# A decoder layer's feed forward in three exact bfloat16 products, behind a survey of the weights, with two key block sets

## The chip, the cores and the metric

The kernel runs on one core of a Trainium2 chip. A core has TensorE (PE, with its weight loads shown apart as PEld), VectorE (DVE), ScalarE (ACT), GpSimd (POOL) and SyncE (SP), which here issues nearly all DMAs. Each engine works through its own queue of instructions in order. The metric is the device time in microseconds (us) of one execution. Lower is better.

## The reference, cut to what matters

One decoder layer on `x` of shape (2, 1024, 256) in float32: causal self attention with rotary embedding, cross attention to 77 context rows, and a gated feed forward. Each is added to its input and followed by a layer norm. All weights of the feed forward are drawn from {-1, 0, 1}; `setup_inputs` multiplies them by 8, and each output row has a float32 scale.

```
x = layernorm(x + self_attention(x))            # 16 heads of 16, causal, rotary
x = layernorm(x + cross_attention(x, ctx))      # ctx: (2, 77, 256)
tlin(x, w, s) = einsum('bsi,oi->bso', x, w) * s
h = silu(tlin(x, w1_w, w1_s)) * tlin(x, w2_w, w2_s)   # 256 -> 1024
h = gelu(tlin(h, h1_w, h1_s))                          # 1024 -> 1024
h = gelu(tlin(h, h2_w, h2_s))                          # 1024 -> 1024
x = layernorm(x + tlin(h, w3_w, w3_s))                 # 1024 -> 256

_ternary(key, shape) = jax.random.randint(key, shape, -1, 2).astype(float32)
factors = {..., 'L0_ffn_w1_w': 8.0, ..., 'L0_ffn_w3_w': 8.0, ...}
```

## The kernel before, in words

Tokens are cut into tiles of 128 (8 per batch) and tiles into five chunks, `CHUNKS` = (batch, first tile, tiles): (0,0,2), (0,2,2), (1,0,4), (0,4,4), (1,4,4). A chunk passes through these steps, each a Python generator whose `yield` gives a pace in microseconds:

- `start` / `project` (L257): per tile, transposes, the query, key and value products, the rotary step on VectorE into a padded tile `qk_pad` (two of them in turn), transposes back. Keys and values go to tiles `kT` and `v` per block of 512 keys, from a pool of 3.
- `top` / `maxima` (L320): scores of each query tile against its earlier keys into the one scores bank `su` (four PSUM banks of 512), and a VectorE reduction (L353) of that bank. The next scores wait for it. The maxima are added to the queries, so the exponentials later need no subtraction.
- `weighted` / `values` (L364): per head group and key tile, transposed scores into `su`, ScalarE's exponential (L400), GpSimd's causal select on the diagonal (L403), and the product with the values into `po`. The value products of one key tile are issued behind the scores of the next.
- `rest`: `self_finish` (L420: division, output projection, residual, norm) and `cross` (L433: the same again on 77 context rows, with its own maxima L461 and exponentials L482).
- `fed` / `feed_forward` (L506): the gate and up layers (tiles `pg`, `pu`), two hidden layers and the last one (`pf`), all with float32 operands. A chunk's weights come as 22 slices of 512 KB from HBM, 5 buffers deep.

The set of scores matmuls for four heads uses four groups of 32 rows of the array at once (`tiled`, L72). All matmuls of the attention are recorded by the helper at L69, those of the feed forward by the helper at L83.

The order is written by hand. `start(0)`, `top(0)`, `weighted(0)` and `cross_keys` (L152) run first, then `rest(0)` beside `start(1)` (`together`, L580: steps are taken by pace). From there on `beside` (L592) takes the attention step by step: maxima of chunk 1, values of chunk 1, then the rest of chunk n together with start and maxima of chunk n+1, values of n+1, and so on. After each step it places feed-forward instructions ("filler") worth the step's pace. The feed forward of a chunk can only begin when its `rest` is done (`attended`), and chunks are fed in order. Filler matmuls may stand at most `AHEAD` = 2 steps ahead of the attention. When the attention is at its end the remaining feed forward runs alone.

Pace of a scores bank in `maxima` is 2.6; of a full key tile in `values` 1.4; of a product of 512 columns in the feed forward 0.86.

## Time and profile before

| | before |
|---|---|
| median of 3 runs | 1361.11 us (1361.1 to 1364.54) |
| the profiled execution, its own time | 1359.41 us |
| its span, first to last instruction | 1357.7 us |
| mean granted TensorE clock | 0.932 |
| busy PE / DVE / ACT / POOL | 1245.1 / 455.4 / 304.9 / 84.0 us |
| DMA moved | 66.19 MB, 14.3% of the span on SP's and ACT's main queue |

How to read the profile: the page has the busy time of each engine, the chain of work that ended last with its shares by engine, groups of instructions by line, operation and shape with their mean, and DMA issues. A float32 matmul appears as two records, each with its own weight load. A busy time can overlap that of the next instruction by the pipeline's depth, so busy times of short groups add up to a little more than the time that they fill. "Stretches" below are a table of the engines' busy time in windows of the span, with the clock that the throttle granted to TensorE (1.00 is full speed).

The first feed-forward matmul starts at 142.4 us, and the last attention matmul ends at 1161.8 us.

### The profile page before, as it was taken

Reading aid. Unit: us, or ns where it says so; the run is one execution under the profiler, and the core shown is the slowest. Engines: PE = TensorE matmul, PEld = TensorE weight load, DVE = VectorE, ACT = ScalarE, POOL = GpSimd, SP = SyncE. Lnnn points to the kernel's source line nnn. Section 1 sums busy time; section 2 is a strip of 40 time slices with the busy share of each in tenths; the row PEclk is TensorE's granted clock in tenths of the full one; section 3 lists DMA queues with packets and bytes.
Section 4 is the critical chain, followed back from the end, with each engine's and each line's share of the span. In section 5 each row is a group of like instructions: output and inputs, shape, how many; then the busy total and the mean of one; then the engine's idle time right before and its main releaser. Section 6 shows DMA issues by size and latency. Waiting matters only on the chain.

```text
span 1357.7 us, 15205 instructions
## 1 busy us (share of the span) xinstructions
PE 1245.1 (92%) x6672; PEld 638.9 (47%) x6672; DVE 455.4 (34%) x705; ACT 304.9 (22%) x328; POOL 84.0 (6%) x131
## 2 busy tenths in 40 slices
PE   6978998898999999998989999899899798999997
PEld 3554646675466755432225544543222343554445
DVE  3133603346133347750003334686000232140002
ACT  1211151211431121004452212010444303011110
POOL 2110011000211000000011000000000000000000
PEclk7585899898899899999999989899899998999999
DMA  5010211122111112110000000111000000122220
GB/s 161 32 47 0 78 48 47 48 78 85 47 61 49 63 47 70 47 63 16 32 31 17 31 31 32 47 47 47 32 31 17 32 26 22 62 92 72 73 74 15
DMA packets 24594, 66.19 MB, mean 49 GB/s; under 512 B 4328, under 2 KB 9553, under 8 KB 24529
## 3 DMA queue, kind: packets, MB, share of 16 engines
q1 hardware_dynamic: 24257, 64.44, 14.3%
q8 instruction: 52, 0.85, 0.3%
q10 hardware_dynamic: 272, 0.79, 0.2%
q14 instruction: 13, 0.11, 0.0%
HBM read 63.12 MB, written 2.10 MB: 48 GB/s over the span
## 4 chain that ended last, share of the span: by engine, by line
PE 82%; ACT 7%; DVE 7%; POOL 2%; issue 2%; DMA 1%; SPq 0%; POOLq 0%; ACTq 0%; DVEq 0%
PE pf L83 36%; PE su L69 18%; PE pm L69 7%; PE po L69 6%; PE pg L83 4%; PE pu L83 4%; ACT pr L400 3%; DVE part L353 2%; PE pq L69 2%; PE pt L226 1%; ACT pr L482 1%; PE pt L235 1%; PE pt L300 1%; DVE top L461 1%; PE pt L246 1%
## 5 line engine op out<-in xcount | busy, mean ns | idle before, releaser
L83 PE MATMUL pf<-nxt,wf 128*128 128x512 f32 (+1 forms) x640 | 251.1, 535 | 0.0
L83 PE MATMUL pf<-hid,wf 128*128 128x512 f32 (+1 forms) x640 | 249.8, 524 | 0.0
L353 DVE TENSOR_REDUCE part<-su 128x4 f32<-128x2048 f32 (+3 forms) x76 | 165.5, 2178 | 76.2 <-PE su L69 75.8
L400 ACT ACTIVATE pr<-su 128x2048 f32<-128x2048 f32 (+1 forms) x104 | 140.6, 1352 | 208.9 <-PE su L69 208.7
L83 PEld LDWEIGHTS pf<-hid,wf 128*128 128x128 f32 x640 | 113.4, 190 | 119.8 <-issue 114.3
L83 PEld LDWEIGHTS pf<-nxt,wf 128*128 128x128 f32 x640 | 122.0, 201 | 98.5 <-issue 91.1
L69 PE MATMUL su<-q,kT 17*128 17x512 f32 (+3 forms) x832 | 97.7, 538 | 26.7 <-ACT pr L400 24.8
L69 PE MATMUL su<-kT,q 16*128 16x128 f32 (+3 forms) x1152 | 92.3, 434 | 12.4 <-DVE part L353 12.1
L546 DVE TENSOR_SCALAR nxt<-pf,sc 128x256 f32<-128x256 f32 (+1 forms) x64 | 39.4, 615 | 181.6 <-PE pf L83 181.0
L69 PE MATMUL po<-pr,v 128*32 128x512 f32 (+3 forms) x832 | 90.5, 510 | 2.0 <-POOL pr L403 1.5
L69 PEld LDWEIGHTS su<-q,kT 17*128 17x128 f32 x832 | 35.6, 197 | 90.1 <-ACT pr L400 59.1
L417 DVE COPY osb<-po 128x512 f32<-128x512 f32 (+1 forms) x20 | 11.7, 585 | 186.7 <-PE po L69 186.7
L403 POOL TENSOR_SCALAR_AFFINE_SELECT pr<-pr 128x512 f32<-128x512 f32 x64 | 40.6, 635 | 513.6 <-ACT pr L400 513.6
L69 PEld LDWEIGHTS su<-kT,q 16*128 16x128 f32 x1152 | 45.7, 205 | 51.9 <-DVE part L353 25.9
L83 PE MATMUL pg<-xTc,wf 128*128 128x512 f32 (+1 forms) x160 | 69.2, 552 | 0.3 <-DVE xTc L218 0.3
L83 PE MATMUL pu<-xTc,wf 128*128 128x512 f32 (+1 forms) x160 | 65.8, 530 | 0.1
L530 ACT ACTIVATE gate<-pg,sc 128x512 f32<-128x512 f32 (+1 forms) x40 | 24.1, 601 | 185.2 <-PE pg L83 185.1
L83 PE MATMUL pf<-wf,nxt 128*128 128x256 f32 x256 | 58.4, 385 | 0.0
L548 ACT ACTIVATE nxt<-nxt 128x1024 f32<-128x1024 f32 (+1 forms) x16 | 23.7, 1483 | 134.1 <-DVE nxt L546 133.9
L83 PEld LDWEIGHTS pf<-wf,nxt 128*128 128x128 f32 x256 | 48.7, 193 | 9.0 <-issue 1.6
L565 DVE TENSOR_TENSOR o<-pf,s 128x256 f32<-128x256 f32 x16 | 6.8, 423 | 134.8 <-PE pf L83 134.8
L482 ACT ACTIVATE pr<-su 77x2048 f32<-77x2048 f32 (+1 forms) x20 | 30.6, 1531 | 64.2 <-PE su L69 64.2
(103 smaller groups left out, 1018.9 us busy)
## 6 DMA issues: line engine op xcount, KB each, us to landing
wf<-in_wf_dram SPq DMA_DIRECT2D x110, 512.0 KB, 3.2
x<-in_x_dram SPq DMA_DIRECT2D x16, 128.0 KB, 3.4
out_dram<-x SPq DMA_DIRECT2D x16, 128.0 KB, 1.8
wqkv<-in_w_qkv_dram ACTq DMA_DIRECT2D x1, 768.0 KB, 4.9
wk<-in_wkT_dram SPq DMA_DIRECT2D x1, 512.0 KB, 5.2
wq<-in_wqT_dram SPq DMA_DIRECT2D x1, 512.0 KB, 3.5
rope<-in_rope_dram SPq DMA_DIRECT2D x1, 256.0 KB, 5.1
wproj<-in_w_proj_dram SPq DMA_DIRECT2D x1, 256.0 KB, 5.0
```

The costliest lines, as they stand in the source:

```text
L69: latest[0] = nc.tensor.matmul(*args, **kw).ins
L83: ins = nc.tensor.matmul(*args, **kw).ins
L226: nc.tensor.transpose(pt[:, g * P : (g + 1) * P], m_pad[:, 4 * g : 4 * g + 4, :].rearrange("p h d -> p (h d)"), ident)
L235: nc.tensor.transpose(pt[:, g * P : (g + 1) * P], osb[:, g, i * P : (i + 1) * P], ident)
L246: nc.tensor.transpose(pt[:, k * P : (k + 1) * P], y[:, k * P : (k + 1) * P], ident)
L353: nc.vector.tensor_reduce(part[:, m, g0 : g0 + gm, :].rearrange("p g j -> p j g"), su[:, :, : gm * r].rearrange("p j (g r) -> p j g r", g=gm),
L400: nc.scalar.activation(pr[:, :, q0:], su[:, :, q0 : n * P], AF.Exp)
L403: nc.gpsimd.affine_select(out=pr[:, :, q0 : q0 + P], in_=pr[:, :, q0 : q0 + P], compare_op=ALU.is_ge, fill=0.0, base=0, pattern=[[0, 4], [ ...
L482: nc.scalar.activation(pr[:L], su[:L, :, : n * P], AF.Exp)
L530: nc.scalar.activation(gate, pg, AF.Tanh, scale=sc[:, 0, f : f + 1])
L546: nc.vector.tensor_scalar(nxt[:, f, :], pf, sc[:, s, f : f + 1], None, ALU.mult)
L548: nc.scalar.activation(nxt[:, f - 3 : f + 1, :], nxt[:, f - 3 : f + 1, :], AF.Gelu)
```

## The change

- **Survey.** While the first chunk's attention runs, all 22 weight slices are loaded once. VectorE takes the maximum of the low 16 bits of every float32 word (L704 of the changed kernel), ScalarE copies the high 16 bits as a bfloat16 tile (L706), and SP stores that to a scratch tensor `wh` in HBM (L707). One matmul against ones and a comparison turn the maxima into a flag: 0 if every weight is exact in bfloat16.
- **Branch.** Every engine loads the flag (L800) and branches (L815). On 0 it runs `feed_forward_exact`, else the float32 `feed_forward`. All that stands behind, the attention of the chunks from 1 on included, is in both sides; pools for it are opened anew inside each side (`part`).
- **Three products.** Activations x stay float32 in `hid`; `split` takes the upper half-word as the first bfloat16 plane, subtracts it on VectorE (L606), copies the upper half of what is left into a bfloat16 tile on ScalarE (L608), and writes the last remainder into the lower half-words of x (L609). The three planes sum to x. Each float32 matmul becomes three bfloat16 ones with the same weight block, of which the first and last plane are read in steps of four bytes. Where a layer begins (`first`) two outputs are summed together, the early blocks first, then plane by plane.
- **Pace.** A pair of bfloat16 products has the pace 0.43 for 512 columns, so the filler is again placed by its time.
- **Order and buffers.** The chunks are now (0,0,2), (0,2,2), (0,4,4), (1,0,4), (1,4,4). Keys and values have two fixed sets (`kT`, `v`), used by one batch and then by the other. Queries have two fixed tiles, and cross attention's queries `qx` take the tile of the chunk's own queries. There is one `qk_pad` instead of two.

```diff
-CHUNKS = ((0, 0, 2), (0, 2, 2), (1, 0, 4), (0, 4, 4), (1, 4, 4))
+CHUNKS = ((0, 0, 2), (0, 2, 2), (0, 4, 4), (1, 0, 4), (1, 4, 4))
...
-    for i in range(2):
+    for i in range(1):
         pad = wself.tile([P, 2, H, 32], F32, name=f"qk_pad{i}")
...
-    kT, v = {}, {}
+    kT = [keys.tile([P, NG, KB], F32, name=f"kT{i}") for i in range(NT // KT)]
+    v = [keys.tile([P, KT, H * DV + 16], F32, name=f"v{i}") for i in range(NT // KT)]
+    for i in range(NT // KT):
+        nc.gpsimd.memset(v[i], 1.0)
+    qs = [queries.tile([P, NG, KB], F32, name=f"q{i}") for i in range(2)]
...
-    def cross(b, t0, n):
+    def cross(b, t0, n, qx):
         x1T = yield from transposed_tokens(b, t0, n)
-        qx = queries.tile([P, NG, n * P], F32, tag="q", name="qx")
...
+    def word_halves(x):
+        both = x.bitcast(BF16).rearrange("p k (n two) -> p k n two", two=2)
+        return both[..., 1], both[..., 0]
+
+    def planes_of(x, mid):
+        upper, lower = word_halves(x)
+        return upper, mid, lower
+
+    def split(x, mid, k0, k1):
+
+        upper, lower = word_halves(x)
+        left = pl.acts.tile([P, k1 - k0, x.shape[-1]], F32, tag="left", name="left", bufs=2)
+        nc.vector.tensor_tensor(left, x[:, k0:k1, :], upper[:, k0:k1, :], ALU.subtract)
+        left_upper = word_halves(left)[0]
+        nc.scalar.copy(mid[:, k0:k1, :], left_upper)
+        nc.vector.tensor_tensor(lower[:, k0:k1, :], left, left_upper, ALU.subtract)
+
+    def planes_summed(sums, K, step, first):
+
+        if first:
+            early = K // 2 if K > KC else 0
+            runs = [[(p, k) for k in range(early) for p in range(3)]] if early else []
+            runs += [[(p, k) for k in range(early, K)] for p in range(3)]
+        else:
+            runs = [[(p, k) for k in range(K) for p in range(3)]]
+        for r, products in enumerate(runs):
+            for ps, operands in sums:
+                for m, (p, k) in enumerate(products):
+                    filling(
+                        ps,
+                        *operands(p, k),
...
+                    )
+                    if m % 2:
+                        yield 2 * step
+
+    def feed_forward_exact(b, t0, n, alone):
+        slices = slices_of(wh, BF16)
+        N = n * P
+        step = 0.215 * n / KT
+        x2T = yield from transposed_tokens(b, t0, n)
+        xmid = pl.acts.tile([P, KC, N], BF16, tag="xmid", name="xmid")
+        split(x2T, xmid, 0, KC)
+        planes = planes_of(x2T, xmid)
...
+        for f in range(FC):
...
+            for group in [sums] if f == 0 else [[x] for x in sums]:
+                yield from planes_summed(group, KC, step, f == 0)
+            gated(pg, pu, hid, f)
+            if f % 2:
+                split(hid, mid, f - 1, f + 1)
+        for s in (2, 3):
...
+                yield from planes_summed(sums, FC, step, f0 == 0)
+                for f, (pf, _) in zip(fs, sums):
+                    hidden(pf, nxt, s, f, alone)
+                    if alone and f % 2:
+                        split(nxt, nmid, f - 1, f + 1)
+                    elif not alone and f % 4 == 3:
+                        split(nxt, nmid, f - 3, f - 1)
+                        split(nxt, nmid, f - 1, f + 1)
...
+    def survey(flag):
...
+            for i in range(N12 + 2 * NH + N3):
+                w = raw.tile([P, SLICE], F32, tag="w", name="w")
+                nc.sync.dma_start(w, a["wf"][i])
+                low = w.bitcast(U16).rearrange("p (n two) -> p n two", two=2)[..., 0]
+                nc.vector.tensor_reduce(seen[:, i : i + 1], low, AX.X, ALU.max)
+                h = raw.tile([P, SLICE], BF16, tag="h", name="h")
+                nc.scalar.copy(h, w.bitcast(BF16).rearrange("p (n two) -> p n two", two=2)[..., 1])
+                nc.sync.dma_start(wh[i], h)
+                yield 1
...
-    run(start(0))
-    run(top(0))
-    run(weighted(0))
-    run(cross_keys())
...
+    with part():
+        run(start(0))
+        run(together((chain(top(0), weighted(0), cross_keys(), attention()), 1.0), (survey(flag), 0.8)))
+    other_weights = nc.values_load(flag, min_val=0, max_val=1)
...
+    with tc.If(other_weights == 0) as exact:
+        beside_each_other(feed_forward_exact, 5)
+    with exact.Else():
+        beside_each_other(feed_forward, 4)
```

Here `attention()` issues the remaining loads of `x` and of the scales and runs `rest(0)` beside `start(1)`, and `beside_each_other` holds what followed it: the maxima of chunk 1 and all later steps beside the feed forward.

## The prediction

> **What bounds the kernel now.** I read the page first (busy shares, the chain that ended last), then a table of stretches cut where the attention changes its step, then single instructions in order of time, then the groups by shape. From the page:
>
> ```profile
> PE 1245.1 (92%) x6672; PEld 638.9 (47%) x6672; DVE 455.4 (34%) x705; ACT 304.9 (22%) x328; POOL 84.0 (6%) x131
> ...
> PE 82%; ACT 7%; DVE 7%; POOL 2%; issue 2%; DMA 1%; SPq 0%; POOLq 0%; ACTq 0%; DVEq 0%
> ```
>
> TensorE is the bound, in work and on the chain. The table of stretches (us, then busy time of PE, PEld, DVE, ACT, POOL; then granted clock, DMA share, GB/s):
>
> ```profile
> 40.00:68.00 28.00, 28.00 (x178) 15.71 (x171) 1.61 (x5) 9.05 (x18) 5.07 (x8) 0.50 0.12 40
> 68.00:112.00 44.00, 33.65 (x217) 20.52 (x218) 14.49 (x32) 8.24 (x15) 3.51 (x4) 0.81 0.09 35
> 112.00:142.00 30.00, 24.04 (x130) 12.60 (x128) 13.68 (x21) 1.76 (x3) 0.94 (x2) 0.50 0.00 1
> ...
> 168.00:206.00 38.00, 34.61 (x324) 17.82 (x323) 3.94 (x10) 18.55 (x20) 5.08 (x8) 1.00 0.16 53
> 206.00:338.00 132.00, 117.65 (x798) 85.17 (x800) 61.38 (x104) 21.46 (x34) 7.89 (x10) 0.95 0.20 65
> 338.00:384.00 46.00, 44.08 (x329) 20.77 (x322) 7.06 (x14) 22.40 (x21) 10.16 (x16) 0.93 0.15 50
> 384.00:609.00 225.00, 216.89 (x1191) 125.56 (x1189) 123.66 (x164) 32.74 (x44) 8.54 (x10) 0.97 0.17 56
> 609.00:719.00 110.00, 99.88 (x602) 29.93 (x603) 6.30 (x9) 56.86 (x37) 11.20 (x17) 0.98 0.08 29
> 719.00:953.00 234.00, 220.55 (x1099) 109.69 (x1097) 124.89 (x166) 32.66 (x42) 8.84 (x10) 0.95 0.11 38
> 953.00:1069.00 116.00, 103.94 (x603) 30.62 (x601) 6.29 (x9) 58.77 (x38) 10.16 (x16) 0.94 0.07 25
> 1069.00:1162.00 93.00, 84.23 (x428) 39.99 (x421) 28.96 (x65) 16.41 (x18) 1.26 (x2) 0.96 0.07 23
> 1162.00:1357.70 195.70, 187.61 (x506) 95.06 (x505) 32.15 (x69) 18.41 (x25) 3.77 (x6) 0.99 0.20 67
> ```
>
> Before 142 us there is attention alone, and its clock is half for most of the time, even at 40 to 68 us where PE is busy throughout. From 142 to 1162 us feed-forward (FFN) products fill the attention's gaps and the clock is 0.93 to 1.00. After 1162 us FFN is alone. So FFN does two things here: it costs PE time, and it keeps the clock up. Single instructions (start us, us; the two bf16 lines are two answers for nested windows):
>
> ```profile
> 1226.11 55.10 PE L83 MATMUL pf<-hid,wf 128*128 128x512 f32 x128
> 1281.05 55.10 PE L83 MATMUL pf<-nxt,wf 128*128 128x512 f32 x128
> ...
> 1117.71 0.60 PE L69 MATMUL su<-maskk,ident_h 77*77 77x512 bf16 x2
> 1117.71 0.81 PE L69 MATMUL su<-maskk,ident_h 77*77 77x512 bf16 x3
> ...
> 624.68 1.14 PE L69 MATMUL su<-q,kT 17*128 17x512 f32 x8 [1.06 <-ACT pr L400]
> 625.95 1.88 ACT L400 ACTIVATE pr<-su 128x2048 f32<-128x2048 f32 x1 [1.32 <-PE su L69]
> ```
>
> 128 f32 records take 1281.05 - 1226.11 = 54.94 us, 0.429 each, two to a matmul: 0.858 us for 512 columns. One more bf16 matmul of 512 columns adds 0.81 - 0.60 = 0.21 us. Groups by shape, for VectorE and ScalarE:
>
> ```profile
> L353 DVE TENSOR_REDUCE part<-su 128x4 f32<-128x2048 f32 x32 | 73.2, 2289 | 23.0 <-PE su L69 23.0
> L461 DVE TENSOR_REDUCE top<-su 128x16 f32<-128x1232 f32 x16 | 23.1, 1443 | 52.0 <-PE su L69 52.0
> L290 DVE TENSOR_TENSOR qk_pad<-qk_pad,turned 128x512 f32<-128x512 f32 x2 | 1.4, 689 | 0.0
> L548 ACT ACTIVATE nxt<-nxt 128x1024 f32<-128x1024 f32 x8 | 8.5, 1056 | 59.6 <-DVE nxt L546 59.4
> ```
>
> **The change, part by part.** The sum goes against the profiled execution: span 1357.7, own time 1359.4 (1.7 outside the span), which is 1.7 below the median 1361.1 of the three timed runs.
>
> *Products.* FFN is 704 units of 512 columns (176 per chunk of four token tiles, 88 per chunk of two). f32: 704 x 0.858 = 604 us. Three bf16 products: 704 x 3 x 0.2146 = 453, taking a quarter of the f32 matmul, which the bf16 rows (0.21) support. Bounds: at 0.24 each, what the first of a set costs, 507; at 0.21, 444. Saved: 151 us of PE work. Whether a plane that lies in every second half-word streams as fast, no row shows; f32 rows walk the same four-byte steps at the same 0.2146 per pass, so I take no loss. The Trainium skill (SBUF — State Buffer, on SBUF "cachelines") says a stride is free while two accesses fall in a 16-byte line; here four would, so the page agrees, and no run yet shows it.
>
> *Where it lies.* Counted in the order of both built programs, the tail after the last attention instruction holds 186.3 us of f32 FFN, after it 139.1: that 47 goes wholly. The rest, 418 to 314, is filler within the attention.
>
> *Filler that runs out.* The fillers are paced in microseconds, so each filled step takes what it took, and the filler ends sooner. In the new order chunks 0 and 1 bring 113 us, used up near the end of the maxima of chunk 2, now (0,4,4). Chunk 2's FFN waits until its attention is done. So all of chunk 2's values, its finish and cross attention, and chunk 3's projection and nearly all its maxima run bare. Before, none after 142 us did.
>
> Price of that stretch. Values of a (0,4,4) chunk: 26 units of 512 columns. Bare at full clock a unit is 3.12 us (0.05 wait, 1.19 scores, 1.88 exponential; su start to exp end above), 87 us with the shorter diagonal units' fixed parts. At half clock scores (2 x 1.05) and values (2 x 1.03) take 4.17: PE-bound, 108. I take 108, since the rows at 40 to 68 us show exactly this work at 0.50 with PE full. The Trainium skill (TensorE: Matmul & The Clock Gate, Part 1) says a busy window of some 3.4 us releases the clock. By that the term would be 87; the 28 us row speaks against it. The rest: 46 us of PE at full clock for a four-tile finish and cross (84.2 at 1069 to 1162, less 38.2 in which the products themselves were busy), 31 for projection and maxima of a (1,0,4) chunk (117.7 at 206 to 338, less 63.3 of filler and 23 for a two-tile finish). 77 us, divided by busy share times clock. The bare row 68 to 142 has (33.65 x 0.81 + 24.04 x 0.50)/74 = 0.53; longer instructions should do a little better, 0.58: 133 us. Ends: 92 (0.84) and 197 (0.78 busy at 0.50). Together 241. Filled, the same work's share is what the rows leave beside the filler counted in them: 73 (110 - 37), 58 (93 - 35) and 45 (132 - 56 - 31 for a two-tile finish), 176; so 65 us of the saving go here.
>
> *Survey.* 22 slices: VectorE reads 1024 words each, 1.23 us by the line through 2.289 (2048) and 1.443 (1232); ScalarE copies each, 1.06. 27 and 23 us on engines busy 32 and 22 of the first 116. SP's queue holds loads and stores in turn, and a store waits for its copy; behind the twelfth store stand the two masks' loads, and VectorE's mask conversion stands ahead of the first maximum that the exponentials need. Stepping through the queues with 3.2 us a load, the first maximum lags 2 to 5 us and the first exponential 10 to 12; later slices are loaded in time. I take 12; ends 0 and 40 (all of it on the chain plus waits).
>
> *Branch.* No row shows one. Ends: 0, and 11 (five gaps of "issue" of 2.2 us, the longest on the chain, one for each engine). I take 5, the first weights' landing of about 3 us being in it. The Trainium skill (Runtime: NRT & Kernel Launch, Instruction fetch mechanics) says that a taken branch stalls for an instruction fetch; it gives no figure. The first maxima of chunk 1, overlapped with rest(0) until now, move behind the branch: rest(0) ends 8 earlier, and they cost 6 more later.
>
> *Splits.* Per pair of blocks of 512 columns two VectorE subtractions of 1024 (0.689 + 512 x 1.04 ns = 1.22 each) and a ScalarE copy (1.06). In filled maxima steps PE needs 1.0 + 2.6 = 3.6 us and the reduction 2.3 on VectorE. With the splits VectorE needs, for chunks of four, 2.3 + 0.4 + 1.2 = 3.9 in hidden layers and 2.3 + 1.4 + 1.2 = 5.0 in the first; for chunks of two 3.5 and 5.5. Fourteen first-layer steps cost 1.4 to 1.9 each (23), some 34 others 0.3 (10), and waits for Gelu in VectorE's order about 7: 40 us, half in each filled stretch. Ends: 10 (queue slack) and 100 (every step 5 us). In the tail PE has 10.3 us per pair against 2.4 of each helper; 4 for layer starts. Halved weight traffic, one rotary pad instead of two, the new query and key tiles: 0, since DMA is 9 to 20% busy after 142 us and the fillers cover the pad; without cover (bare stretch) the pad costs up to 1 us a tile, inside the ends above.
>
> *Sum.* To the first product: 138.5 - 8 + 12 + 5 = 148. Filled stretch one: maxima of chunk 1 32 (8 steps of 3.65 and two small ones), its values 38, rest(1) with a long maxima 132 + 58 (16 more steps of 3.65), less 8 for the part without filler, plus 20: 272. Bare: 241. Filled stretch two: 46 + 234 + 116 + 93 as now, plus 20: 509. Tail: 139 + 10 + 4 = 153. Total 1323 + 1.7 = **1325 us**.
>
> **Rivals.**
> - *The bare stretch stays cold* (slower). Half clock throughout: 108 + 197 = 305, total 1389. For it: 112 to 142 us at 0.50. Against: 68 to 112 us at 0.81. It decides from 279 us of bare stretch on, 38 above mine.
> - *VectorE becomes the bound of the filled maxima*: splits cost 100, not 40, total 1385. For it: 123.66 of 225 us busy before any split, in strict order. Against: two steps of slack and idle VectorE elsewhere.
> - *Bare but warm*: 87 + 105 = 192, total 1276. For it: projections raise the clock at 68 to 112 us.
> - *The branch takes the f32 side*: 1361 + 11 for survey and branch + some 45 for a shorter bare stretch, 1415. Against: the weights are -8, 0 or 8.
>
> **How the numbers follow.** Mine 0.52 (own range 1288 to 1352), cold 0.17, VectorE 0.15, warm 0.14, f32 side 0.02. Cutting the outermost tenths: 1272 to 1388. A measurement tells 0.3% (4 us) from no change. Faster 0.52 + 0.14 less the upper edge of mine, 0.64; within 0.3% 0.04; slower 0.32.
>
> **What would show it.** A tail near 153 us with 0.215 per record; a stretch of some 240 us without L91 matmuls and with a clock near 0.6; the first L91 matmul near 148 us; maxima steps in filled stretches above 3.6 us. Wrong if strided planes stream slower than 0.2146, if PE waits at layer starts for the split, or if the bare stretch misses 200 to 280.

## The result and the profile after

The changed kernel takes 1371.33 us (median; 1361.23 to 1378.66) against 1360.85 us of the kernel before, a ratio of 1.0068 with a 95% interval of 1.0048 to 1.0089: slower by 0.7%. The forecast was 1325 us and faster. The time lies inside the forecast range, but the sign of the change is the other one. The profiled execution took 1372.8 us with a span of 1371.0.

The page of the kernel after, with the busy times, the granted clock in 40 slices and the chain that ended last:

```profile
PE 1184.6 (86%) x7542; PEld 577.2 (42%) x7602; DVE 606.2 (44%) x859; ACT 378.9 (28%) x413; POOL 82.1 (6%) x128
...
PEclk8576889987986558965589999999899998899999
...
PE 67%; DVE 17%; ACT 10%; issue 3%; POOL 2%; DMA 1%; SPq 0%; ACTq 0%; POOLq 0%; DVEq 0%
```

TensorE is busy 60.5 us less than before (1245.1), not 151 less, VectorE 151 us more, and VectorE's share of the chain went from 7% to 17%. In the middle, six of eight slices (411 to 685 us) now have a clock of 0.5 to 0.6 and the two between them 0.8 and 0.9; before, only two of the first four slices were at 0.5. The table of stretches of the kernel after, cut where the forecast cut it (us; busy time of PE, PEld, DVE, ACT, POOL; granted clock, DMA share, GB/s):

```profile
0.00:145.00 145.00, 102.92 (x622) 59.88 (x622) 65.60 (x101) 45.05 (x66) 15.15 (x34) 0.69 0.50 167
145.00:438.00 293.00, 255.31 (x2124) 162.21 (x2116) 168.25 (x239) 68.68 (x98) 13.92 (x20) 0.89 0.15 42
438.00:546.00 108.00, 95.31 (x508) 21.75 (x505) 2.08 (x3) 50.19 (x33) 10.16 (x16) 0.59 0.00 1
546.00:692.00 146.00, 117.55 (x649) 61.20 (x647) 58.30 (x100) 17.97 (x27) 7.60 (x8) 0.65 0.00 1
692.00:1211.00 519.00, 466.77 (x2916) 199.71 (x2960) 243.78 (x320) 162.93 (x150) 30.46 (x44) 0.94 0.07 21
1211.00:1371.00 160.00, 146.72 (x741) 72.44 (x752) 68.24 (x98) 34.09 (x40) 4.81 (x6) 0.98 0.15 45
```

Against the forecast (148, 272, 108 and 133, 509, 153): the first product comes 3 us early, the first filled stretch is 21 us long, the values of the bare stretch (the part without feed forward beside the attention) are as long as forecast, its rest is 13 long, the second filled stretch 10 and the tail 7. These make the 48 us between 1323 and 1371. No single stretch holds the miss.

Three details, each from the list of single instructions (start us, us). First, the values of chunk 2 with no feed forward beside them:

```profile
479.75 1.94 PE L77 MATMUL po<-pr,v 128*32 128x512 f32 x8
479.95 1.88 ACT L410 ACTIVATE pr<-su 128x2048 f32<-128x2048 f32 x1 [2.27 <-PE su L77]
...
481.88 2.09 PE L77 MATMUL su<-q,kT 17*128 17x512 f32 x8 [0.19 <-ACT pr L410]
...
483.90 1.94 PE L77 MATMUL po<-pr,v 128*32 128x512 f32 x8
```

A unit takes 483.90 - 479.75 = 4.15 us, with scores at 2.09 and values at 1.94: both are at half clock although TensorE stands still for only some 0.2 us in each. The forecast had 4.17.

Second, VectorE in the first filled stretch, where it works on chunk 2's maxima and chunk 1's first layer:

```profile
328.68 2.28 DVE L363 TENSOR_REDUCE part<-su 128x4 f32<-128x2048 f32 x1
330.87 0.69 DVE L239 TENSOR_TENSOR q<-pt,q 128x512 f32<-128x512 f32 x1
331.47 0.41 DVE L527 SCALAR_TENSOR_TENSOR gate<-gate,pg 128x256 f32<-128x256 f32 x1
331.99 0.48 DVE L528 SCALAR_TENSOR_TENSOR hid<-pu,sc,gate 128x256 f32<-128x256 f32 x1
332.50 0.69 DVE L606 TENSOR_TENSOR left<-hid 128x512 f32<-128x512 f32 x1
333.23 0.75 DVE L609 TENSOR_TENSOR hid<-left 128x512 bf16<-128x512 f32 x1
333.87 2.28 DVE L363 TENSOR_REDUCE part<-su 128x4 f32<-128x2048 f32 x1
```

From one reduction to the next 5.19 us pass, and no line shows idle time in front: VectorE is the bound of this step. The two subtractions of a split (L606, L609) stand between the two reductions.

Third, TensorE in the tail, which reads strided planes (`mid`) twice and a contiguous one (`midm`) once per triple:

```profile
1211.24 0.38 PE L91 MATMUL pf<-midm,wf 128*128 128x512 bf16 x1
1211.46 0.61 PE L91 MATMUL pf<-mid,wf 128*128 128x512 bf16 x2
1211.91 0.38 PE L91 MATMUL pf<-midm,wf 128*128 128x512 bf16 x1
```

A triple takes 0.67 us here (1211.91 - 1211.24), against 3 x 0.2146 = 0.644 in the forecast.

### The profile page after: what moved, and what is told of

The parts are those of the page before. It is cut to its first block, busy times and chain, and to the rows that moved or that the text cites. A ratio compares the mean times of both kernels' runs of the same rounds, so it can differ in the third digit from the quotient of the medians.

```text
span 1371.0 us, 17290 instructions
## 1 busy us (share of the span) xinstructions
PE 1184.6 (86%) x7542; PEld 577.2 (42%) x7602; DVE 606.2 (44%) x859; ACT 378.9 (28%) x413; POOL 82.1 (6%) x128
## 4 chain that ended last, share of the span: by engine, by line
PE 67%; DVE 17%; ACT 10%; issue 3%; POOL 2%; DMA 1%; SPq 0%; ACTq 0%; POOLq 0%; DVEq 0%
PE pf L91 23%; PE su L77 19%; PE pm L77 7%; PE po L77 6%; DVE part L363 5%; ACT pr L410 4%; PE pq L77 2%; PE pu L91 2%; PE pg L91 2%; ACT pr L491 2%; DVE left L606 2%; DVE hid L609 1%; DMA w<-in_wf_dram 1%; PE pt L236 1%; PE pt L245 1%
## 5 line engine op out<-in xcount | busy, mean ns | idle before, releaser
L91 PEld LDWEIGHTS <-wf 128*128 128x128 bf16 x2400 | 229.2, 100 | 270.0 <-issue 111.5
L363 DVE TENSOR_REDUCE part<-su 128x4 f32<-128x2048 f32 (+3 forms) x76 | 165.3, 2175 | 55.0 <-PE su L77 54.7
L91 PE MATMUL pf<-mid,wf 128*128 128x512 bf16 (+1 forms) x625 | 167.4, 355 | 1.7 <-issue 1.2
L91 PE MATMUL pf<-hid,wf 128*128 128x512 bf16 (+1 forms) x620 | 161.8, 345 | 3.1 <-DVE gate L527 0.9
L91 PE MATMUL pf<-midm,wf 128*128 128x512 bf16 (+1 forms) x313 | 102.9, 346 | 0.8 <-issue 0.6
L91 PE MATMUL pf<-hidm,wf 128*128 128x512 bf16 (+1 forms) x313 | 101.3, 339 | 1.6 <-issue 1.4
L427 DVE COPY osb<-po 128x512 f32<-128x512 f32 (+1 forms) x20 | 11.7, 584 | 179.8 <-PE po L77 179.7
L606 DVE TENSOR_TENSOR left<-hid 128x1024 f32<-128x1024 f32 (+1 forms) x40 | 40.0, 1014 | 41.4 <-ACT hid L532 32.1
L91 PE MATMUL pg<-xTc,wf 128*128 128x512 bf16 (+1 forms) x157 | 50.7, 375 | 1.7 <-DVE xTc L228 0.9
L608 ACT COPY hidm<-left 128x1024 bf16<-128x1024 bf16 (+1 forms) x40 | 34.9, 875 | 58.1 <-DVE left L606 57.7
L91 PE MATMUL pu<-xTc,wf 128*128 128x512 bf16 (+1 forms) x156 | 50.3, 374 | 0.6 <-issue 0.5
L470 DVE TENSOR_REDUCE top<-su 128x16 f32<-128x1232 f32 x16 | 23.1, 1442 | 54.2 <-PE su L77 54.2
```

What stands on the lines that cost most here:

```text
L91: ins = nc.tensor.matmul(*args, **kw).ins
L363: nc.vector.tensor_reduce(part[:, m, g0 : g0 + gm, :].rearrange("p g j -> p j g"), su[:, :, : gm * r].rearrange("p j (g r) -> p j g r", g=gm),
L470: nc.vector.tensor_reduce(top.rearrange("p g j -> p j g"), su[:, :, : NG * L].rearrange("p j (g l) -> p j g l", g=NG), AX.X, ALU.max,)
L606: nc.vector.tensor_tensor(left, x[:, k0:k1, :], upper[:, k0:k1, :], ALU.subtract)
L608: nc.scalar.copy(mid[:, k0:k1, :], left_upper)
```

## The experiments

Runs are compared by the ratio to runs of the kernel before on the same chip, whose medians went from 1359.9 to 1365.7 us between groups. Stretches are compared at marks that all runs with the new order share: first product, last reduction (L363) of chunk 2, first product after the bare stretch, last reduction (L470) of the cross attention, end. In the float32 run and the one with the slower pace, products still run to 491 and 480 us, so their column "bare" is not bare to that point. Between the marks the kernel after has these (first, middle two, last):

```profile
145.00:435.00 290.00, 253.09 (x2113) 161.19 (x2106) 167.56 (x238) 68.68 (x98) 13.92 (x20) 0.89 0.15 43
435.00:692.00 257.00, 215.08 (x1164) 83.97 (x1163) 61.07 (x104) 68.16 (x60) 17.76 (x24) 0.63 0.00 1
692.00:1161.00 469.00, 422.34 (x2718) 181.50 (x2760) 228.11 (x290) 147.50 (x137) 30.46 (x44) 0.95 0.08 22
1161.00:1371.00 210.00, 191.16 (x940) 90.66 (x953) 83.91 (x129) 49.52 (x53) 4.81 (x6) 0.95 0.13 37
```

| run | ratio to before (95%) | to first product | filled one | bare | filled two | end |
|---|---|---|---|---|---|---|
| after | 1.0068 (1.0048 to 1.0089) | 145 | 290 | 257 | 469 | 210 |
| after, again | 1.0085 (1.0061 to 1.0109) | 146 | 287 | 250 | 469 | 210 |
| float32 in this frame | 1.0507 (1.0461 to 1.0552) | 151 | 270 | 245 | 440 | 311 |
| no splits | 0.9633 (0.9603 to 0.9662) | 145 | 270 | 248 | 436 | 208 |
| copies of the split only | 0.9569 (0.9529 to 0.9608) | 144 | 270 | 244 | 442 | 206 |
| contiguous planes | 1.0023 (0.9994 to 1.0052) | 148 | 290 | 252 | 464 | 208 |
| no branch | 0.9999 (0.9976 to 1.0022) | 148 | 289 | 248 | 467 | 208 |
| splits on GpSimd | none | 148 | 270 | 250 | 473 | 217 |
| dummy products, two | 0.9885 (0.9839 to 0.9931) | 146 | 290 | 232 | 467 | 210 |
| slower pace | 0.9872 (0.9826 to 0.9919) | 148 | 262 | 248 | 437 | 253 |

### The products alone: float32 in the new frame

```
-    with tc.If(other_weights == 0) as exact:
-        beside_each_other(feed_forward_exact, 5)
-    with exact.Else():
-        beside_each_other(feed_forward, 4)
+    beside_each_other(feed_forward, 4)
```

> The changed kernel with its survey, its new order and its two sets of keys, but the float32 feed forward always, and no branch. Theory A (in this order the products' saving is given back because filler that is 25% cheaper leaves more of the attention bare): 1345 to 1375 us, so that the exact products gain at most a few us here, or lose. Theory B (the exact products keep most of their 151 us and the loss is the order's and the survey's): 1415 us or more, 45 above the changed kernel.

Measured 1425.24 us (1418.32 to 1436.8): theory B. So the frame (survey, new order, two key sets) costs 5.1% by the ratio and some 65 us by the medians, and the exact products take back about 54 of them. Of the 65, 9 fall ahead of the first product (151 us instead of 142.4), where the survey lies; the survey, the order and the key sets are not separated here. The forecast had a loss of this size in its "float32 side" rival (1415). The stretches of this run:

```profile
151.00:421.00 270.00, 250.16 (x1634) 168.34 (x1628) 130.34 (x171) 47.51 (x67) 12.96 (x18) 0.94 0.22 70
421.00:666.00 245.00, 209.73 (x1292) 97.41 (x1291) 67.39 (x120) 76.60 (x67) 18.88 (x26) 0.79 0.07 21
666.00:1106.00 440.00, 415.68 (x2316) 179.14 (x2313) 169.51 (x237) 115.58 (x108) 30.39 (x44) 0.97 0.11 34
1106.00:1416.60 310.60, 297.22 (x825) 142.00 (x823) 49.03 (x104) 34.40 (x37) 3.76 (x6) 0.97 0.19 63
```

In the two filled stretches float32 takes 270 and 440 us, the exact products 290 and 469: they are slower there, by 20 and 29 us. Nearly all that they gain is the 101 us at the end, where the float32 filler that found no place in the attention is done alone.

### The splits

Without splits:

```
     def planes_of(x, mid):
         upper, lower = word_halves(x)
-        return upper, mid, lower
+        return upper, upper, upper
     def split(x, mid, k0, k1):
+        return
```

> The changed kernel without the splits into planes: all three products of a triple use the upper half-words, so 60 instructions of VectorE of 1.0 us or more and as many copies of ScalarE are left out, and the feed forward's activations keep only their upper halves. Theory A (splits slow the filled maxima through VectorE): the two filled stretches shrink by 15 to 25 us each, the tail by 4, to 1320 to 1340 us. Theory B (VectorE has slack there, and the 20 and 9 us above the forecast are the strided products): below 8 us less, 1363 us or more.

ScalarE's copies kept, VectorE's subtractions left out:

```
-        return upper, mid, lower
+        return upper, mid, upper
...
-        left = pl.acts.tile(...)
-        nc.vector.tensor_tensor(left, x[:, k0:k1, :], upper[:, k0:k1, :], ALU.subtract)
-        left_upper = word_halves(left)[0]
-        nc.scalar.copy(mid[:, k0:k1, :], left_upper)
-        nc.vector.tensor_tensor(lower[:, k0:k1, :], left, left_upper, ALU.subtract)
+        nc.scalar.copy(mid[:, k0:k1, :], upper[:, k0:k1, :])
```

> The changed kernel with ScalarE's copy of a split kept, of the activations' upper half-words, and both of VectorE's subtractions left out, so that the planes are the upper half-words twice and their copy. Theory A (the splits' 63 us are VectorE's time in the order of its maxima): as without splits, 1305 to 1320 us. Theory B (they are ScalarE's time in the order of its exponentials, or the wait for the plane at the start of a layer): 1340 us or more.

Measured 1308.58 us (1306.94 to 1314.99) and 1307.62 us (1302.03 to 1307.93). Theory A, and further: without splits the kernel is below the lower end that theory A gave. With the copies it is no slower, so ScalarE's 65 copies cost nothing that shows, and what the splits cost comes from VectorE's subtractions: their time, or the wait for their results. Without splits the two filled stretches take 270 and 436 us, as with float32 (270 and 440). The same two reductions as above, in the run without splits:

```profile
324.64 2.29 DVE L363 TENSOR_REDUCE part<-su 128x4 f32<-128x2048 f32 x1
326.85 0.68 DVE L239 TENSOR_TENSOR q<-pt,q 128x512 f32<-128x512 f32 x1
327.45 0.41 DVE L527 SCALAR_TENSOR_TENSOR gate<-gate,pg 128x256 f32<-128x256 f32 x1
327.96 0.48 DVE L528 SCALAR_TENSOR_TENSOR hid<-pu,sc,gate 128x256 f32<-128x256 f32 x1
328.37 2.28 DVE L363 TENSOR_REDUCE part<-su 128x4 f32<-128x2048 f32 x1
```

3.73 us instead of 5.19: the step is shorter by 1.46 us, and the subtractions took 0.69 and 0.75.

Then both subtractions on GpSimd (`nc.vector` becomes `nc.gpsimd` in the two lines):

> The changed kernel with both subtractions of a split on GpSimd, which is busy 6% of the time, instead of VectorE. Theory A (the 63 us that the splits cost are VectorE's, in whose order they stand between the maxima): 1310 to 1335 us, and a VectorE of some 480 us of busy time. Theory B (the cost is the time from a layer's last sum to its planes, whoever makes them): no gain, 1365 us or more, since GpSimd takes longer over 1024 words than VectorE's 1.01 us.

The times spread from 1343.69 us at a mean clock of 0.864 to 1368.4 at 0.838, so no ratio is given; the profiled execution took 1359.41. That lies between the ranges of the two theories, and in the stretches each holds for a part. The first filled stretch falls to 270 us, all that the splits cost there: it was VectorE's order. The second stays at 473 and the end grows by 7. The chain within the second filled stretch (by line, cut off at the right by the view), first of the kernel after, then of the run with GpSimd:

```profile
by line: PE pf L91 24.9%; PE su L77 18.0%; PE po L77 7.3%; PE pm L77 5.9%; DVE part L363 5.8%; PE pu L91 3.6%; DVE left L606 3.4%; ACT pr L410 3.0%; issue 2.8%; PE pg L91 2.8%; DVE hid L609 2.0%; PE pq L77 1.5%; PE pt L236 1.5%; ACT mid L53
```

```profile
by line: PE pf L91 28.1%; PE su L77 18.3%; PE po L77 8.0%; PE pm L77 5.9%; POOL left L606 5.6%; PE pg L91 3.1%; PE pu L91 3.1%; issue 2.8%; DVE part L363 2.6%; ACT pr L410 1.8%; ACT mid L536 1.6%; POOL mid L609 1.6%; PE pq L77 1.5%; PE pt L
```

And the first subtraction of the hidden layers' splits in the same two runs (count; least, median and longest time in ns; first and last start in us; shapes):

```profile
L606 DVE TENSOR_TENSOR left<-hid x40: 681/1219/1414, 153.8 to 1351.8; 128x1024 f32<-128x1024 f32 x24, 128x512 f32<-128x512 f32 x16
```

```profile
L606 POOL TENSOR_TENSOR left<-hid x40: 1040/1894/1897, 157.6 to 1338.2; 128x1024 f32<-128x1024 f32 x24, 128x512 f32<-128x512 f32 x16
```

Taking the subtractions off VectorE halves the reductions' share of the chain (5.8% to 2.6%), but on GpSimd one of 1024 columns takes 1.89 us instead of 1.22 (the 1.01 of VectorE in the expectations is a mean over 1024 and 512 columns), and the subtractions themselves stand on the chain with 7.2% of 473 us, some 34, where on VectorE they had 5.4% of 469, some 25. So by the chain the next layer waits for its planes in this stretch, whoever makes them; no run takes that wait away and leaves VectorE's order as it is.

### Stride and branch

Planes read from the contiguous tile only:

```
-        return upper, mid, lower
+        return mid, mid, mid
```

> The changed kernel with the splits kept, but all three products of a triple read the middle plane, which lies contiguous; the upper and the lower plane are left out of the sums. Theory A (a plane in every second half-word streams 5% slower, 0.226 against 0.213 us per 512 columns): 10 to 18 us less, 1353 to 1361 us, and a triple of 0.64 us in the tail. Theory B (the 0.013 is the switch between planes and not the stride): the triple stays at 0.665, and the time within 3 us of 1371.

The feed-forward products without the branch:

```
-    with tc.If(other_weights == 0) as exact:
-        beside_each_other(feed_forward_exact, 5)
-    with exact.Else():
-        beside_each_other(feed_forward, 4)
+    beside_each_other(feed_forward_exact, 5)
```

> The changed kernel without its branch: the exact feed forward always, the survey kept with its flag unread. Theory A (the branch is small, as the forecast had it at 5 us): 0 to 6 us less, 1365 to 1371 us, all of it ahead of the first product at 145.45 us. Theory B (the branch also costs later, by code that is no longer fetched in time): more than 10 us less, spread over the stages.

Contiguous planes: 1361.12 us (1357.6 to 1373.6), at the edge of theory A by its median. Products in the tail of that run, and then of the run without splits, whose triple reads one strided plane three times:

```profile
1261.65 2.54 PE L91 MATMUL pf<-hidm,wf 128*128 128x512 bf16 x11
```

```profile
1239.75 3.55 PE L91 MATMUL pf<-hid,wf 128*128 128x512 bf16 x15
```

Less the 0.38 of a single one, that is 0.216 a product from the contiguous plane and 0.226 from the strided one. The strided run has no switch between planes either, so theory B's switch is not the cause: the stride is.

No branch: 1364.33 us (1359.26 to 1381.92), by the ratio 0.7% below the kernel after, yet its stretches are the same within 3 us, but for the bare one (248 instead of 257). What differs is the granted clock. The single runs of the kernel after go from 1361.8 us at a mean clock of 0.860 to 1378.5 at 0.846, and at 0.858 to 0.860 they read 1361.2 to 1364.1; those without a branch 1359.3 to 1366.2, with contiguous planes 1357.6 and 1357.7 at 0.860. A straight line through the 29 runs of the kernel after (10.3 us for 0.01 of clock) leaves the runs without a branch 2.6 us below it in the mean and those with contiguous planes 5.4. So at equal clock the branch costs 2 to 3 us at most, which is near what can be told here, and the stride some 5 us.

### The bare stretch

The feed forward's steps declared a third longer, so that the filler is dealt out as the float32 one was:

```
-        step = 0.215 * n / KT
+        step = 0.287 * n / KT
...
-            yield from planes_summed(sums, FC, 0.107, i0 == 0)
+            yield from planes_summed(sums, FC, 0.143, i0 == 0)
```

> The changed kernel with the exact feed forward's steps declared a third longer, so that it is dealt out to the attention at the pace of the float32 one and lasts as long. Theory A (the saving is given back because the cheaper filler runs out 106 us earlier than the float32 one does in this order, 278 us against 172 without filler): the stretch without filler shrinks to 170 to 190 us, the tail grows by 40 to 50 us, and the time is 1330 to 1350 us. Theory B (VectorE, with the splits, sets the filled stretches, and spreading only leaves TensorE idle in them): 1365 us or more.

1349.3 us (1340.74 to 1351.49): theory A, at its upper end. The stretch without any product is 178 us (480 to 658) instead of 266 (426 to 692; the expectation counted 278, from 414 on, where products still ran), and the end takes 253 instead of 210. The filled stretches shrink as well, by 28 and 32 us; less filler and fewer splits fall in them, which this run doesn't separate.

Two bfloat16 products that nobody reads at each step where the feed forward has nothing ready, then one:

```
-                credit -= next(filler, None) or credit
+                pace = next(filler, None)
+                if pace is None:
+                    warm()
+                credit -= pace or credit
+    def warm():
+        ps = bank("warm").rearrange("p (g n) -> p g n", g=NG)
+        for _ in range(2):
+            filling(ps, ident_h, causal..., start=True, stop=True)
```

> The changed kernel with two bfloat16 products of 512 columns, whose sums nobody reads, at every step of the attention at which the feed forward has nothing ready. They add 0.43 us of TensorE's work a step and compute nothing. Theory A (the stretch without filler is long because its clock is 0.59 and 0.65): the clock in it rises to 0.9 or more, its values take 87 to 95 us instead of 108 and the rest 100 to 115 instead of 146, and the time is 1305 to 1330 us. Theory B (the waits between engines set that stretch, or the added products cost what the clock gives): 1360 us or more.

> The run with dummy products, with one product of 512 columns a step instead of two: 0.21 us of TensorE's work, still computing nothing. With two, the values of the stretch without filler took 95 us at a clock of 0.95 instead of 114 at 0.60, but the rest 152 us at 0.88 instead of 158 at 0.67. Theory A (the rest is short of clock, and two dummies cost what the clock gave): the clock stays above 0.85 and the rest falls to 130 to 142 us. Theory B (the rest is set by waits between engines, whatever the clock): 148 to 158 us. Theory C (one dummy a step is too little to hold the clock): clock below 0.75 there, and times as in the changed kernel.

With two: 1348.97 us (1342.48 to 1352.34), between the theories. Every stretch but the bare one is as in the kernel after; that one falls from between 250 and 257 us to 232, and its clock rises to 0.91. Single instructions of its values:

```profile
450.08 1.14 PE L77 MATMUL su<-q,kT 17*128 17x512 f32 x8 [0.52 <-ACT pr L410]
...
451.16 1.07 PE L77 MATMUL po<-pr,v 128*32 128x512 f32 x8
451.35 1.88 ACT L410 ACTIVATE pr<-su 128x2048 f32<-128x2048 f32 x1 [1.32 <-PE su L77]
...
452.15 0.61 PE L91 MATMUL warm<-causal,ident_h 128*128 128x512 bf16 x2
...
453.28 1.14 PE L77 MATMUL su<-q,kT 17*128 17x512 f32 x8 [0.52 <-ACT pr L410]
```

Scores take 1.14 instead of 2.09 us, a unit 3.20 instead of 4.15, and the bound is no longer TensorE but the way through the one scores bank: scores (1.14), then ScalarE's exponential (1.88), then the next scores. Doing useless work made the attention faster: for the values the cold clock is shown to be the cause. With one dummy a step, 1363.4 us (1357.36 to 1375.92), a ratio of 1.0034 (1.0009 to 1.0058). The values and the rest of that run:

```profile
435.00:549.00 114.00, 103.01 (x565) 24.90 (x565) 3.46 (x5) 50.20 (x33) 10.16 (x16) 0.69 0.00 1
549.00:702.00 153.00, 134.74 (x787) 67.55 (x788) 70.88 (x111) 22.78 (x33) 7.60 (x8) 0.78 0.01 2
```

The clock stops halfway, at 0.69 and 0.78, and the times stay at 114 and 153 us: nearest to theory C, though the rest lies in theory B's range as well. For the rest (finish, cross attention, projection, maxima) two dummies gave 152 us at 0.88, one 153 at 0.78, none 158 and 155 at 0.67 and 0.70. With two, TensorE is busy with dummies alone for 40 of its 152 us.

The kernel after itself shows more, when its bare stretch is cut where its clock changes (columns as above):

```profile
428.00:520.00 92.00, 82.27 (x404) 19.89 (x403) 6.87 (x12) 36.72 (x24) 7.28 (x12) 0.50 0.01 5
520.00:540.00 20.00, 13.84 (x121) 3.43 (x113) 0.69 (x1) 11.43 (x8) 1.90 (x3) 1.00 0.00 1
540.00:547.00 7.00, 6.52 (x44) 2.07 (x44) 0.00 (x0) 2.05 (x3) 1.90 (x3) 0.54 0.00 0
547.00:592.00 45.00, 35.25 (x207) 21.12 (x200) 20.87 (x45) 8.99 (x19) 6.33 (x6) 0.99 0.00 1
592.00:697.00 105.00, 86.08 (x450) 41.49 (x451) 41.66 (x59) 10.02 (x9) 1.27 (x2) 0.50 0.00 1
```

So attention alone is not always cold: most of the last head group's values, and then the finish with the start of the cross attention, run at full clock with nothing beside them. What released the clock there, and took it back at 592 us, no run shows. It fits the mixed result of the dummies. From the copy behind the last values (L427) to the last cross-attention maximum (L470), 63 and 66 us pass in the two profiled executions of the kernel after, and 73 with two dummies. From there to chunk 3's last long maximum (L363) it is 96 and 89 us, against 80. The dummies cost time where the clock was up and gave time where it was half. What that last part would take at full clock with nothing beside it stays open.

### Order and pace

The old order, with a third set of keys and values; the room for it comes from `left`, `gate` (one buffer each) and the weights (three):

```
-CHUNKS = ((0, 0, 2), (0, 2, 2), (0, 4, 4), (1, 0, 4), (1, 4, 4))
+CHUNKS = ((0, 0, 2), (0, 2, 2), (1, 0, 4), (0, 4, 4), (1, 4, 4))
...
+    SETS = ((0, 2), (1, 0))
```

> The changed kernel with the old order of chunks, (1,0,4) ahead of (0,4,4), and therefore three sets of keys and values; to make room the exact feed forward has three weight buffers and one buffer each for its gate and its remainders. Theory A (the order makes the filler run out): in the old order the values of a (0,4,4) chunk and the rest between chunks 2 and 3 have filler again, so the bare stretch of 278 us without filler shrinks to below 60 us, and the time falls to 1310 to 1330 us, faster than the kernel before by 2.5 to 3.5%. Theory B (the loss is in the products themselves: the stride of four bytes, the splits): the order moves the bare stretch but the time stays at 1355 to 1375 us.

1353.87 us (1352.56 to 1359.16), a ratio of 0.995 (0.9934 to 0.9967). Theory A missed: the bare stretch does not go below 60 us, it falls into three, in the rest of each chunk of four and the projection behind it:

```profile
480.00:564.00 84.00, 66.96 (x271) 26.18 (x268) 29.20 (x43) 10.27 (x9) 1.26 (x2) 0.50 0.00 0
...
840.00:922.00 82.00, 66.49 (x266) 26.11 (x264) 28.14 (x41) 10.27 (x9) 1.26 (x2) 0.50 0.00 0
...
1187.00:1223.00 36.00, 23.83 (x75) 11.46 (x76) 10.27 (x32) 3.88 (x6) 2.52 (x4) 0.59 0.06 22
```

These are 202 us, nearly all at half clock; counted from product to product, the three gaps are 228 us (471 to 568, 833 to 925, 1186 to 1225). Both orders run dry with the cheaper filler at the same pace. So the old order and the slower pace together, and then with one subtraction of each split (`lower`) and with both on GpSimd:

> The old order of chunks with three sets of keys, and the exact feed forward's steps declared a third longer: the order and the pace of the kernel before with the new products. Theory A (with filler everywhere the saving is kept): no stretch above 20 us without filler, a tail of some 160 us against 196 before, and 1310 to 1335 us. Theory B (VectorE sets the filled steps, with the splits in its order, so cheaper filler makes them no shorter and TensorE idles): the stretches before the tail take as long as before or longer, and the time is 1340 us or more.

> As the last, with the second of a split's two subtractions on GpSimd. Theory A (VectorE's 60 subtractions in the order of the maxima are what the filled stretches lose): 10 to 20 us less than the last run. Theory B (the way from a layer's last sum to its planes is what they lose; GpSimd takes 1.56 us for it, VectorE 1.01): the same within 6 us or more time.

> The old order and the slower pace with both subtractions of a split on GpSimd. Theory A (every subtraction taken out of VectorE's order is a gain): 1290 to 1300 us, another 5 to 15 below the run with one on GpSimd at 1305. Theory B (with both there, the 2 x 1.56 us delay the planes at layer starts and the causal masks that GpSimd makes for the values): 1305 to 1320 us.

1315.95 us (1313.81 to 1326.42), 0.9662 (0.9603 to 0.9722); 1305.36 us (1303.46 to 1314.03), 0.9586 (0.9537 to 0.9634); 1314.74 us (1313.18 to 1316.97), 0.9666 (0.9649 to 0.9684). All three beat both kernels. The first fits theory A in its time; one subtraction on GpSimd brings 10.6 us more by the medians (A, at its lower end; four runs each, and the intervals still overlap), and the second takes most of them back (B). In the first of the three the filler lasts from 147 to 1305 us with no gap above 12. Where its VectorE is loaded, theory B has a part: the maxima of the (0,4,4) chunk, in that run and then in the kernel before:

```profile
463.00:611.00 148.00, 125.32 (x822) 57.87 (x829) 101.61 (x113) 29.23 (x31) 2.22 (x4) 0.92 0.10 27
```

```profile
470.00:608.00 138.00, 134.75 (x721) 65.49 (x719) 85.54 (x96) 19.16 (x20) 2.22 (x4) 1.00 0.17 56
```

TensorE has 9 us less to do there, VectorE 16 more, and the stretch is 10 us longer. Of the 44 us between the spans of the kernel before and this version (1357.7 and 1314.2), 39 come after its last cross-attention reduction (203 us from 1111 to 1314, against 242 from 1116 to 1358).

The kernel after, once more on the chip of the last runs:

> The changed kernel itself, unaltered, on the chip of the two other runs, so that they are compared with it there. Both theories: 1362 to 1376 us, 0.3 to 1% above the kernel before.

1371.12 us (1361.79 to 1378.46), as both expected.

## Why the prediction was wrong, point by point

- **Products.** 0.67 us a triple, not 0.644: the step "I take no loss" for strided planes failed. Measured, a strided plane takes 0.226 us a product, a contiguous one 0.216. The Trainium skill (SBUF — State Buffer, on SBUF "cachelines") has a stride free while two accesses fall in one 16-byte line; here four do, and the measurement decides against it, by less than 5%. It was worth some 5 us of time. In the tail, 139 us of products at 0.67 in place of 0.644 make 5 of the 7 that it is long (an estimate).
- **Filler that runs out.** Right in mechanism and place: no products from 426 to 692 us, as the forecast had it ("all of chunk 2's values, its finish and cross attention, and chunk 3's projection and nearly all its maxima").
- **Price of the bare stretch.** The values took 108 us between the cuts and 111 from their first scores (436.68) to their last product (547.3), so the 108 forecast was close, but in part by luck. The forecast had half clock throughout. One of the four head groups took 28.7 us at half clock (465.12 to 493.84, from first scores to first scores), which would make 115 for four; the last group, mostly at full clock, took 25.5 and brought it back. The choice of the row at 40 to 68 us over the rule was right: from 428 to 520 us TensorE was busy for 82 of 92 us and the clock stayed at 0.50. The Trainium skill (TensorE: Matmul & The Clock Gate, Part 1) has a busy window of some 3.4 us release the clock. By that the values would have taken 87; the row of 92 us speaks against it, and with dummy products they came near it (95). The rest took 146, not 133. The step "longer instructions should do a little better, 0.58" failed: busy share times clock was 117.55 / 146 x 0.65 = 0.52, what the nearest row (0.53) had said. Of the rows behind that term, the filler at 206 to 338 us is 62.2 us in the trace, not 63.3, a slip of 1.
- **Survey and branch.** 12 and 5 forecast; the first product came at 145 to 148 us, and at 148 in the run without the branch. So the branch shows no cost here, and the two together took 15 to 18 us of the 17 forecast, if the sum's start holds; the 5 given to the branch then belong to the survey, or to the 8 that the overlap's end was to bring. That start, 138.5, stands in no row: the first product of the kernel before is at 142.4. No run shows whether the branch had to fetch instructions that were not at hand, which is the case in which the Trainium skill (Runtime: NRT & Kernel Launch, Instruction fetch mechanics) speaks of a stall.
- **Splits.** Forecast 40, half in each filled stretch, and 4 in the tail. Measured between the marks: 17 to 20 in the first, 27 to 33 in the second, 2 to 4 at the end; by the times of the runs without them, over 60 in all. What is left of the 60 lies in the bare stretch (2 to 13 us), which has no split and differs by 7 us between two executions of the kernel after itself. The mechanism was right, and so was the first half's size. The second half was mis-sized: besides the queue of VectorE there is the next layer's wait for its planes, which the run with GpSimd has on the chain and which the sum had only in the tail. The DMA share that the forecast reads as 9 to 20% is 7 to 20% in its rows; nothing hangs on it.
- **Filled stretch one.** With 20 for splits measured as forecast, the 18 us left are an error in the base: float32 in the new frame takes 270 us up to chunk 2's last reduction, and so do the exact products without splits; the sum had 252. Two terms are likely. A long step was put at 3.65 us; in the run without splits eleven in a row (347.2 to 392.8 us, from reduction to reduction) take 4.15 each, which makes 8 over the sum's 16 more steps (an estimate). And "less 8 for the part without filler" found no such gain: products last to 426 of the 435 us, and the 15 us without them (304 to 319) had a clock of 0.65. How the 18 divide is not shown.
- **"The fillers are paced in microseconds, so each filled step takes what it took."** Right, and shown by the same two 270s. But the reading stopped short: it also means that a quarter less work in the filler makes no filled step shorter. What it saves shows only at the end (311 us with float32, 210 after), and against the kernel before that did not pay for the frame. A slower pace alone gave 27 us in the new order and 39 in the old, by the ratios.
- **The rivals.** "VectorE becomes the bound of the filled maxima" was half of it (over 60 us, between 44 and 100). "The bare stretch stays cold" did not happen as a whole: 254 us, short of its 279, and 65 us of it at full clock. "Bare but warm" did not come about even with dummy products: 232 us, not 192.

So the forecast of a gain failed in the sizes of terms, not in one step: filled stretch one 293 instead of 272 (nearly all of it in the base), the bare rest 146 instead of 133, filled stretch two 519 instead of 509 (the second half of the splits), the tail 160 instead of 153 (mostly the strided planes). Only the start was 3 short. An expected gain of 36 us met a miss of 48. That the time still fell into the wide range is no merit of the sum.

## What to carry to other kernels

Where filler is dealt out by a declared cost, cheaper filler does not make the work it accompanies shorter; it ends sooner. Declare the cost anew so that it lasts (here worth 27 to 39 us), and count what it costs to be without it: attention alone ran at half clock for three quarters of its bare stretch, so that even useless products beside it shortened the stretch. Count the helper instructions of a trick (here two subtractions per pair of blocks) on the engine whose order sets the steps, and again as latency between one layer's last sum and the next layer's first product.

## What the runs showed of the hardware that was not expected

- Attention alone stayed at half clock for 92 us with TensorE busy for 82 of them (4.15 us units at 0.50), yet the same work ran at full clock for the 20 us that followed, with TensorE busy for 14. Two bfloat16 products of 512 columns per step brought the values to a mean of 0.95; one per step only to 0.69.
- The time of the kernel after goes with its granted clock from run to run: 1361.8 us at 0.860, 1378.5 at 0.846. It spreads more (1.2%) than the kernel before (0.5% on the same chip), and medians a few us apart say little unless the clocks are compared.
- The same subtraction of 1024 float32 words took 1.22 us on VectorE and 1.89 on GpSimd, and with one of two on each the kernel was faster (1305 us) than with both on GpSimd (1315) and, by the medians, than with both on VectorE (1316).
- A moving bfloat16 plane read in steps of four bytes took 0.226 us for 512 columns, a contiguous one 0.216.
